# Last depthwise unit of a fused convolution kernel: results loaded in halves, an affine formed ahead, three weights issued later, a sigmoid by Exp

## The chip, the cores and the metric

The kernel runs on one core of a Trainium2 chip. The metric is device time in microseconds of one execution; the runs shown are the median of three. A profile is one further execution, recorded by the hardware profiler. The engines are PE (TensorE, matmuls; PEld are its weight loads), DVE (VectorE), ACT (ScalarE), POOL (GpSimd) and SP (SyncE, which only issues DMAs). ACT and POOL issue DMAs too. L1425 is line 1425 of the kernel before.

## The reference, cut to what matters

Four layers work on x of shape (4, 384, 64, 64) in float32; each is x + f(gn(x)), with gn a group norm. The change lies in layer 2:

```python
# layer 2, on x after the group norm; bn is a norm over batch and pixels, per channel
kw = softmax(bn(...))                       # two numbers for each batch, from the means of x
y3 = bn(depthwise 3x3 of x)
y5 = bn(depthwise 5x5 of x)
y1 = x * c1_w + c1_b                        # per channel
tok = bn(kw0 * y3 + kw1 * y5 + y1)
gp = tok.mean(over pixels)
gh = gelu(bn(gp @ cg_w1))
gates = sigmoid(bn(gh @ cg_w2))             # one number for each batch and channel
tok = tok * gates
h1 = gelu(bn(tok @ cm_w1)); h2 = bn(h1 @ cm_w2)
out = gate * (tok + h2) + (1 - gate) * x
```

Layer 0 is an attention, layer 1 a filter in the frequency domain, layer 3 a dynamic depthwise 7x7 convolution; they are not touched.

## The kernel before, in words

The kernel is one program of four phases. `phase_a` computes layers 0 and 1. `phase_b` computes the two depthwise convolutions of layer 2 and the sum tok before its norm. `phase_ef` forms tok's norm and the gates and does the two dense products of layer 2. `phase_g` does layer 3. A tile framework decides the order of the instructions on each engine from priorities and dependencies, and sets the semaphores; a DMA waits, by a ring of eight completion semaphores, for one some eight DMAs earlier. Each engine, and SP's queue of DMAs, works strictly in its order.

`phase_b` works in twelve units of 32 channels. For a unit, 16 steps of `conv53` do two channels each: TensorE multiplies strips of the image (z) with Toeplitz matrices made from the taps (L1425), ACT copies both results out of PSUM (L1434, L1436), DVE takes statistics (L1439), and after every fourth step ACT issues a store of 1 MiB (L1441) to a scratch tensor d in DRAM. So a unit has four such stores; that of steps 0 to 3 holds its channels 0 to 7, and so on. The layout in the unit is by image row, so the results come back by channel: `load_results` (L1482) reads a quarter of the rows of all 32 channels and 4 batches in one DMA of 1 MiB to 128 partitions (partition = 32 x batch + channel, pieces of 1 KiB).

`conv_norms` turns the statistics into the factors s (for the two convolutions) and the offset s0. `unit_tok` (L1491) then forms tok for a unit, in four parts of 1024 pixels: ACT forms x * c1_w + s0 for 512 pixels into PSUM (L1503), DVE adds the one convolution's result (L1512) and then the other's with a sum over the pixels (L1514), into x's own buffer; for each 1024 pixels ACT squares with a sum (L1524), and issues a store of tok (L1531, 512 KiB). For all units but the last this is spread over the steps of the next unit's convolutions. The results go into a pool of three buffers (`bc_p`), and the fourth load waits for the first to be free. For the last unit there is no next one. Its four results are loaded after its last store, into buffers of `bx_p` (six buffers of 8 KiB in each partition, which also hold x of three units, two buffers each), and `unit_tok` runs alone:

```python
            self.results = [self.load_results(UNITS - 1, i, self.bx_p, "x") for i in range(4)]
            self.conv_norms(UNITS - 1, behind)
            for _ in self.unit_tok(UNITS - 1):
                pass
            self.tok_stats()
```

`tok_stats` (L1533) sums up. At its start `phase_ef` issues three weights from ACT (L1601 to L1603, by `weight`, L335): cm_w1 (1.15 MiB), cg_w1 (36 KiB) and cg_w2 (36 KiB). Then come tok's norm (`bn_scale_shift`, with L374 Ln and L375 Exp for the inverse root), the matmuls with cg_w1 (L1613) and cg_w2 (L1620, with statistics L1622 and L1623), the sigmoid (L1627), and its products with the norm's scale and offset, at and ct (L1630, L1631). Sigmoid is not in the table of functions that holds Ln and Exp, so ACT loads a table before it and `ln_exp` loads the other again after it (L344).

The blocks of the dense product follow: SP loads tok for 1024 pixels (L1655, e_tok for two thirds of the channels and a part of z for the last third, in DMAs of 32 partitions and 128 KiB) and x (L1665, e_x, 1.5 MiB), DVE applies at and ct (L1656) and scales e_x (L1684), and TensorE multiplies with cm_w1 (h_s, L1671). 16 such blocks take about 500 us.

Of the kernel before, what the change touches and what calls it, by code (L numbers as in the profile page):

```python
# [30 lines left out]
P = 128  # L31
# [251 lines left out]
class _Builder:  # L283
# [930 lines left out]
    def phase_b(self):  # L1214
# [5 lines left out]
        with ExitStack() as ctx:  # L1220
# [13 lines left out]
            self.unit_x = [[] for _ in range(UNITS)]  # L1234
            first, strips, behind = self.unit_strips(0), self.unit_strips(1), None
            next(first)
            for u in range(UNITS):
                st = self.bt_p.tile([P, 2, 16, 6], F32, tag="st", name="st")
                tok = self.unit_tok(u - 1) if u else first
                for n in range(16):  # L1240
# [19 lines left out]
                    if not u and n in (1, 3):  # L1260
                        next(strips)
                    if n == 14 and not u:
                        for _ in tok:
                            pass
# [8 lines left out]
                behind, before = st, tok  # L1273
            self.results = [self.load_results(UNITS - 1, i, self.bx_p, "x") for i in range(4)]
            self.conv_norms(UNITS - 1, behind)
# [206 lines left out]
    def load_results(self, u, i, pool=None, tag="d"):  # L1482
# [6 lines left out]
        return d  # L1489

    def unit_tok(self, u):  # L1491

        nc = self.nc
        s, s0 = self.tok_s
        results, self.results = self.results, None
        behind = None
        for i in range(4):
            d = results[i]
            o = self.unit_x[u][i // 2][:, i % 2 * 1024 : i % 2 * 1024 + 1024]
            for h in range(2):  # L1500
                part = slice(h * 512, (h + 1) * 512)
                m = self.psum.tile([P, 512], F32, tag="t", name="tok_m", bufs=2)
                nc.scalar.activation(  # L1503
                    m, o[:, part], AF.Identity, bias=s0, scale=self.vec("c1_w")[:, u : u + 1]
                )
                if h == 0 and behind is not None:
                    self.square_and_store(u, *behind)
                    if len(results) == 3:
                        results.append(self.load_results(u, 3))
                mv, ov = (t.rearrange("p (y n) -> p y n", n=P) for t in (m, o[:, part]))  # L1510
                of = lambda v: d[:, 4 * h : 4 * h + 4, v]
                nc.vector.scalar_tensor_tensor(mv, of(1), s[:, 1:2], mv, ALU.mult, ALU.add)  # L1512
                k = 2 * i + h
                nc.vector.scalar_tensor_tensor(  # L1514
                    ov, of(0), s[:, 0:1], mv, ALU.mult, ALU.add, accum_out=self.total[:, u, k : k + 1]
                )
                yield
            behind = i, d, o
        self.square_and_store(u, *behind)

    def square_and_store(self, u, i, d, o):

        nc = self.nc
        nc.scalar.activation(  # L1524
            d.rearrange("p y v n -> p (y v n)")[:, 0:1024],
# [65 lines left out]
    def phase_ef(self, strips):  # L1591
        tc, nc = self.tc, self.nc
        with ExitStack() as ctx:
# [6 lines left out]
            io = first.enter_context(tc.tile_pool(name="e_io", bufs=2))  # L1600
            w1 = self.weight(ep, "cm_w1_t")  # L1601
            cg1 = self.weight(ep, "cg_w1_t")
            cg2 = self.weight(ep, "cg_w2_t")  # L1603

# [14 lines left out]
            for j in range(NJ):  # L1619
# [3 lines left out]
                nc.vector.bn_aggr(mv[:, j], st)  # L1623
            ga, gc = self.bn_scale_shift("cg2", mv[:, :, 0], mv[:, :, 1], self.vec("cg_g2"), self.vec("cg_b2"))
            for j in range(NJ):
                gates = self.sm([P, B], "gates")
                last = nc.scalar.activation(  # L1627
                    gates, z[:, j], AF.Sigmoid, bias=gc[:, j : j + 1], scale=ga[:, j : j + 1]
                )
                nc.vector.tensor_scalar(self.at[:, j, :], gates, a[:, j : j + 1], None, ALU.mult)  # L1630
                nc.vector.tensor_scalar(self.ct[:, j, :], gates, c[:, j : j + 1], None, ALU.mult)  # L1631


            self.ln_exp(last)
            stay = self.sm([P, B], "stay")
# [719 lines left out]
```

## Time and profile before

| what | value |
|---|---|
| time, median of 3 runs | 4648.23 us (4632.54 to 4652.59) |
| the profiled execution's own time | 4666.46 us |
| its span, first to last instruction | 4664.7 us |
| granted TensorE clock, mean | 0.969 |
| PE busy | 4356.6 us, 93% of the span |
| DVE, ACT, POOL busy | 61%, 43%, 17% |
| last conv store issued (L1441) | at 2969.97 us |
| first of the four c_d loads issued (L1485) | at 2973.88 us |
| last sum of unit_tok ends (L1514) | at 2998.13 us |
| first matmul of h_s (L1671) | at 3016.59 us |

Times inside the execution count from the start of its span. [...]the share is an average over stages, so the stretch around the change has to be read by itself. In rows of a timeline the engine's name with a q behind it is its sequencer, which issues the DMAs.

### The profile page before, as it was taken

The page shows a single profiled execution, that of the slowest core. Times are in us where ns is not written, and L with a number is a line of the kernel's source. Part 1 is how long each engine was busy: PE and PEld are TensorE (multiplying, and loading weights), DVE is VectorE, ACT ScalarE, POOL GpSimd, SP SyncE. Part 2 cuts the span into 40 slices and gives each one's busy share as a digit, 9 for nine tenths or more (in the row PEclk, how much of TensorE's full clock was granted, in tenths as well). Part 3 has the DMA queues.
Part 4 walks back from the last instruction along what each step waited for, and adds up shares of the span by engine and source line. Part 5 has one row for each costly group of instructions (what it writes and reads, how often), then busy time and mean ns, then how long its engine had stood idle before and what let it go on. Part 6 is the DMA issues. An engine that isn't in the chain of part 4 may idle for free.

```text
span 4664.7 us, 49796 instructions
## 1 busy us (share of the span) xinstructions
PE 4356.6 (93%) x18445; PEld 2415.0 (52%) x18445; DVE 2856.1 (61%) x4680; ACT 1991.0 (43%) x2913; POOL 810.8 (17%) x784
## 2 busy tenths in 40 slices
PE   7899999999999999998988899699999999888998
PEld 2233444334443444443538898444444444588987
DVE  6766566655666445554877888755541113777898
ACT  3444344444444443343535666411115333664442
POOL 1000000000000000000005566200000000245764
PEclk9999999999999999998989999799999999998999
DMA  4301211111111211112317999866655333796896
GB/s 141 114 33 50 84 68 68 53 63 48 61 68 46 71 37 59 50 61 82 127 64 248 315 336 331 298 257 254 257 225 212 140 144 134 280 348 234 264 316 223
DMA packets 284320, 730.36 MB, mean 157 GB/s; under 512 B 22331, under 2 KB 122790, under 8 KB 272806
## 3 DMA queue, kind: packets, MB, share of 16 engines
q1 hardware_dynamic: 213096, 407.56, 27.4%
q0 software_dynamic: 38880, 173.96, 9.9%
q10 hardware_dynamic: 32094, 145.57, 7.8%
q8 instruction: 149, 2.44, 0.2%
q14 instruction: 101, 0.83, 0.1%
HBM read 433.13 MB, written 293.86 MB: 156 GB/s over the span
## 4 chain that ended last, share of the span: by engine, by line
PE 70%; DVE 14%; DMA 8%; issue 3%; ACT 3%; POOL 1%; SPq 0%; ACTq 0%; DVEq 0%; POOLq 0%
PE av L933 11%; PE h_m L1792 11%; PE h_s L1671 11%; PE conv_m L1425 5%; PE sc_s L815 5%; PE proj_m L969 4%; DVE acc L1138 4%; PE t_m L1059 4%; PE conv_m L2187 3%; PE av L838 3%; PE out_m L1162 2%; PE out_m L1161 2%; PE back_m L1084 2%; DMA in_raw<-raw 2%; DMA x_in<-in_x 1%
## 5 line engine op out<-in xcount | busy, mean ns | idle before, releaser
L823 ACT ACTIVATE probs<-sc_s 128x1024 f32<-128x1024 f32 x512 | 497.2, 1021 | 698.5 <-PE av L933 597.9
L933 PE MATMUL av<-probs,vt 128*128 128x512 f32 x1536 | 723.9, 608 | 0.0
L1138 DVE SCALAR_TENSOR_TENSOR acc<-band,vecs,acc 128x512 f32<-128x512 f32 x708 | 496.2, 745 | 44.8 <-POOL band L1097 39.7
L1425 PE MATMUL conv_m<-toep,z 128*128 128x192 f32 (+1 forms) x2304 | 446.5, 351 | 21.7 <-DVE z L1354 11.9
L933 PEld LDWEIGHTS av<-probs,vt 128*128 128x128 f32 x1536 | 279.0, 193 | 343.3 <-issue 339.6
L1792 PE MATMUL h_m<-f_h,cm_w_t 128*128 128x512 f32 x1008 | 436.1, 595 | 7.4 <-ACT f_h L1729 7.4
L1425 PEld LDWEIGHTS conv_m<-toep,z 128*128 128x128 f32 x2304 | 402.6, 195 | 45.5 <-ACT d_o L1436 15.5
L2187 PE MATMUL conv_m<-toep,z 128*128 128x128 f32 x3072 | 383.7, 282 | 23.3 <-DVE toep L2174 13.8
L2187 PEld LDWEIGHTS conv_m<-toep,z 128*128 128x128 f32 x3072 | 370.3, 199 | 25.9 <-DVE toep L2174 10.0
L1671 PE MATMUL h_s<-e_tok,cm_w_t 128*128 128x512 f32 x768 | 362.8, 595 | 4.1 <-DVE e_tok L1656 4.1
L1792 PEld LDWEIGHTS h_m<-f_h,cm_w_t 128*128 128x128 f32 x1008 | 192.4, 191 | 250.6 <-issue 240.0
L815 PE MATMUL sc_s<-q,k 32*128 32x512 f32 x2048 | 307.2, 642 | 15.4 <-ACT probs L823 15.3
L1406 POOL TENSOR_TENSOR toep<-w,band 128x1280 f32<-128x1280 f32 x96 | 278.3, 2899 | 200.0 <-PE conv_m L1425 187.6
L1059 PE MATMUL t_m<-w_in_t,xb 128*128 128x384 f32 x768 | 281.1, 501 | 2.6 <-DVE coef L1076 2.4
L969 PE MATMUL proj_m<-xm,w_proj_t 128*128 128x512 f32 x576 | 271.2, 610 | 5.7 <-DVE xm L908 4.9
L1678 ACT COPY e_h<-h_s 128x1024 f32<-128x1024 f32 x96 | 97.3, 1013 | 400.1 <-PE h_s L1671 400.1
L1680 DVE BATCH_NORM_STATS2 h_st<-e_h 128x6 f32<-128x512 f32 x192 | 123.5, 685 | 219.3 <-ACT e_h L1678 219.3
L1671 PEld LDWEIGHTS h_s<-e_tok,cm_w_t 128*128 128x128 f32 x768 | 146.5, 191 | 188.2 <-issue 183.5
L976 DVE SCALAR_TENSOR_TENSOR x_res<-proj_m,bn_c,x_res 128x512 f32<-128x512 f32 x96 | 71.7, 747 | 241.0 <-PE proj_m L969 240.9
L1059 PEld LDWEIGHTS t_m<-w_in_t,xb 128*128 128x128 f32 x768 | 143.6, 193 | 141.3 <-issue 62.8
L1671 PE MATMUL h_s<-z,cm_w_t 128*128 128x512 f32 x384 | 196.7, 594 | 0.0
L838 PE MATMUL av<-probs,vt 128*32 128x512 f32 x1536 | 188.6, 603 | 4.6 <-DVE av_t L867 4.6
(464 smaller groups left out, 6336.4 us busy)
## 6 DMA issues: line engine op xcount, KB each, us to landing
d<-d_o ACTq DMA_DIRECT2D x48, 1024.0 KB
c_d<-d SPq DMA_DIRECT2D x48, 1024.0 KB
hid<-e_h ACTq DMA_DIRECT2D x16, 3072.0 KB
f_h<-hid SPq DMA_DIRECT2D x14, 3072.0 KB
x_in<-in_x SPq DMA_DIRECT2D x96, 256.0 KB
x_res<-in_x SPq DMA_DIRECT2D x32, 768.0 KB
xa<-x_res POOLq DMA_DIRECT2D x32, 768.0 KB, 3.7
xa_out<-xa SPq DMA_DIRECT2D x32, 768.0 KB
```

Of the source, the lines that this page charges most:

```text
L815: nc.tensor.matmul(s[:, g], lhsT=k4[32 * g : 32 * g + 32, c], rhs=q[i][32 * g : 32 * g + 32], start=True, stop=True,)
L823: nc.scalar.activation(p[:, h * 1024 : (h + 1) * 1024], s[:, 2 * h : 2 * h + 2].rearrange("p a b -> p (a b)"), AF.Exp, scale=0.25,)
L838: nc.tensor.matmul(av[k][quarter(g)], lhsT=vt[:, 4 * c + v, quarter(s)], rhs=p[:, v * 512 : (v + 1) * 512], start=c == 0 and not before, s ...
L933: nc.tensor.matmul(av[0], lhsT=vt[:, 4 * c + v, :], rhs=p[:, v * 512 : (v + 1) * 512], start=c == 0 and v == 0, stop=c == 7 and v == 3,)
L969: nc.tensor.matmul(m, lhsT=self.w_proj[:, j, o * P : (o + 1) * P], rhs=xm[:, j], start=j == 0, stop=j == NJ - 1,)
L1059: nc.tensor.matmul(m[:, 0:C], lhsT=xb[:, j], rhs=self.w_in[:, j, :], start=j == 0, stop=j == NJ - 1,)
L1138: nc.vector.scalar_tensor_tensor(out, src(j, k), w, done, ALU.mult, ALU.add)
L1406: eng.tensor_tensor(t, self.w53[:, at : at + 160].rearrange("p (m n) -> p m n", n=8).unsqueeze(2).to_broadcast([P, 20, 8, 8]), band.rearra ...
L1425: nc.tensor.matmul(m[:, c * 256 + to : c * 256 + to + 64 * (k1 - k0)], lhsT=self.z_[:, at : at + P], rhs=t[:, 10 * c + k0 : 10 * c + k1].r ...
L1671: nc.tensor.matmul(s[:, v, :], lhsT=w1[:, j, o * P : (o + 1) * P], rhs=t[j][:, v * 512 : (v + 1) * 512], start=j == 0, stop=j == NJ - 1,)
L1792: nc.tensor.matmul(m, lhsT=w2[:, o, j * P : (j + 1) * P], rhs=h[o][:, v * 512 : (v + 1) * 512], start=o == 0, stop=o == 5,)
L2187: nc.tensor.matmul(m[:, ch % 4 * P : (ch % 4 + 1) * P], lhsT=self.z_[:, at : at + P], rhs=t[:, 8 * c + 2 * i : 8 * c + 2 * i + 2].rearrang ...
```

## The change

In the last unit the four results are loaded in two halves of the channels. `load_half` reads 16 of the 32 channels, with one DMA for each batch: 16 partitions, 8 rows of 1 KiB each, 128 KiB. The first halves (channels 0 to 15, stored after steps 3 and 7) are put into the program after steps 8, 9, 12 and 15 of the last unit, into the same `bx_p` buffers; the second halves take the place of the old loads. So four DMAs become 32 of the same bytes in total. For the last unit, x * c1_w + s0 is formed ahead of the parts, in place in x's buffer and for 1024 pixels at a time; DVE then adds to it in place, and PSUM is not used. The three weights of `phase_ef` are issued from ACT behind the last unit's third square, the two small ones first. The sigmoid becomes 1 / (1 + exp(-v)): scale and offset are negated on DVE, ACT runs Exp, DVE adds one and takes the reciprocal; both table loads go.

```diff
--- before.py
+++ after.py
@@ -1232,7 +1232,7 @@
             for n in range(LEAD + 2):
                 self.matrices53(n)
             self.unit_x = [[] for _ in range(UNITS)]
-            first, strips, behind = self.unit_strips(0), self.unit_strips(1), None
+            first, strips, behind, last = self.unit_strips(0), self.unit_strips(1), None, []
             next(first)
             for u in range(UNITS):
                 st = self.bt_p.tile([P, 2, 16, 6], F32, tag="st", name="st")
@@ -1259,6 +1259,10 @@
                         next(tok, None)
                     if not u and n in (1, 3):
                         next(strips)
+                    if u == UNITS - 1 and n in (8, 9, 12, 15):
+                        last.append(self.bx_p.tile([P, 2 * 8 * P], F32, tag="x", name="c_d"))
+                        d = last[-1] = last[-1].rearrange("p (y v n) -> p y v n", v=2, n=P)
+                        self.load_half(u, len(last) - 1, d, 0)
                     if n == 14 and not u:
                         for _ in tok:
                             pass
@@ -1271,7 +1275,9 @@
                         if n == 15:
                             strips = coming
                 behind, before = st, tok
-            self.results = [self.load_results(UNITS - 1, i, self.bx_p, "x") for i in range(4)]
+            self.results = last
+            for d, i in zip(self.results, range(4)):
+                self.load_half(UNITS - 1, i, d, 1)
             self.conv_norms(UNITS - 1, behind)
             for _ in self.unit_tok(UNITS - 1):
                 pass
@@ -1488,21 +1494,39 @@
         )
         return d
 
+    def load_half(self, u, i, d, half):
+
+        at = 16 * half
+        for b in range(B):
+            self.nc.sync.dma_start(
+                d[32 * b + at : 32 * b + at + 16].rearrange("p y v n -> p y (v n)"),
+                self.d53[u][8 * i : 8 * i + 8, b, at : at + 16].rearrange("y c v n -> c y (v n)"),
+            )
+
     def unit_tok(self, u):
 
         nc = self.nc
         s, s0 = self.tok_s
         results, self.results = self.results, None
-        behind = None
+        behind, last = None, u == UNITS - 1
+        if last:
+            for x in self.unit_x[u]:
+                for k in range(2):
+                    x_k = x[:, k * 1024 : k * 1024 + 1024]
+                    nc.scalar.activation(
+                        x_k, x_k, AF.Identity, bias=s0, scale=self.vec("c1_w")[:, u : u + 1]
+                    )
         for i in range(4):
             d = results[i]
             o = self.unit_x[u][i // 2][:, i % 2 * 1024 : i % 2 * 1024 + 1024]
             for h in range(2):
                 part = slice(h * 512, (h + 1) * 512)
-                m = self.psum.tile([P, 512], F32, tag="t", name="tok_m", bufs=2)
-                nc.scalar.activation(
-                    m, o[:, part], AF.Identity, bias=s0, scale=self.vec("c1_w")[:, u : u + 1]
-                )
+                m = o[:, part]
+                if not last:
+                    m = self.psum.tile([P, 512], F32, tag="t", name="tok_m", bufs=2)
+                    nc.scalar.activation(
+                        m, o[:, part], AF.Identity, bias=s0, scale=self.vec("c1_w")[:, u : u + 1]
+                    )
                 if h == 0 and behind is not None:
                     self.square_and_store(u, *behind)
                     if len(results) == 3:
@@ -1511,17 +1535,18 @@
                 of = lambda v: d[:, 4 * h : 4 * h + 4, v]
                 nc.vector.scalar_tensor_tensor(mv, of(1), s[:, 1:2], mv, ALU.mult, ALU.add)
                 k = 2 * i + h
-                nc.vector.scalar_tensor_tensor(
+                self.last_sum = nc.vector.scalar_tensor_tensor(
                     ov, of(0), s[:, 0:1], mv, ALU.mult, ALU.add, accum_out=self.total[:, u, k : k + 1]
                 )
                 yield
             behind = i, d, o
+        self.third_square = self.last_square
         self.square_and_store(u, *behind)
 
     def square_and_store(self, u, i, d, o):
 
         nc = self.nc
-        nc.scalar.activation(
+        self.last_square = nc.scalar.activation(
             d.rearrange("p y v n -> p (y v n)")[:, 0:1024],
             o,
             AF.Square,
@@ -1598,9 +1623,10 @@
             first = ctx.enter_context(ExitStack())
             ep = first.enter_context(tc.tile_pool(name="e_const", bufs=1))
             io = first.enter_context(tc.tile_pool(name="e_io", bufs=2))
-            w1 = self.weight(ep, "cm_w1_t")
-            cg1 = self.weight(ep, "cg_w1_t")
-            cg2 = self.weight(ep, "cg_w2_t")
+            with tc.issue_after(self.third_square.ins):
+                cg1 = self.weight(ep, "cg_w1_t")
+                cg2 = self.weight(ep, "cg_w2_t")
+                w1 = self.weight(ep, "cm_w1_t")
 
             a, c = self.bn_scale_shift("bn_ar", *self.over_batches("ar", self.mvt), self.vec("ar_g"), self.vec("ar_b"))
             gp = self.sm([P, NJ, B], "gp")
@@ -1622,16 +1648,17 @@
                 nc.vector.bn_stats(st, z[:, j])
                 nc.vector.bn_aggr(mv[:, j], st)
             ga, gc = self.bn_scale_shift("cg2", mv[:, :, 0], mv[:, :, 1], self.vec("cg_g2"), self.vec("cg_b2"))
+            for v in (ga, gc):
+                nc.vector.tensor_scalar(v, v, -1.0, None, ALU.mult)
             for j in range(NJ):
                 gates = self.sm([P, B], "gates")
-                last = nc.scalar.activation(
-                    gates, z[:, j], AF.Sigmoid, bias=gc[:, j : j + 1], scale=ga[:, j : j + 1]
-                )
+                nc.scalar.activation(gates, z[:, j], AF.Exp, bias=gc[:, j : j + 1], scale=ga[:, j : j + 1])
+                nc.vector.tensor_scalar(gates, gates, 1.0, None, ALU.add)
+                nc.vector.reciprocal(gates, gates)
                 nc.vector.tensor_scalar(self.at[:, j, :], gates, a[:, j : j + 1], None, ALU.mult)
                 nc.vector.tensor_scalar(self.ct[:, j, :], gates, c[:, j : j + 1], None, ALU.mult)
 
 
-            self.ln_exp(last)
             stay = self.sm([P, B], "stay")
             nc.vector.tensor_scalar(stay, self.gate, -1.0, 1.0, ALU.mult, ALU.add)
             self.gx, self.gn, self.gh, self.g0 = (self.coef(k) for k in ("gx", "gn", "gh", "g0"))
```

`issue_after` places an instruction behind a given one in its engine's order.

## Prediction

> **What bounds the kernel now.** I read the windows view first: where is TensorE idle around the change? Columns: stretch, its length, then busy time and count for PE, PEld, DVE, ACT and POOL, granted clock, DMA share, GB/s.
>
> ```profile
> 2970.00:3016.60 46.60, 4.64 (x25) 3.73 (x25) 23.73 (x82) 18.97 (x34) 0.58 (x1) 0.54 0.97 300
> 3016.60:3513.00 496.40, 496.40 (x1151) 219.73 (x1152) 259.14 (x406) 96.98 (x96) 11.28 (x16) 1.00 0.66 244
> ```
>
> For 46.6 us TensorE has almost nothing to do; then it is full for 496 us at a DMA share of 0.66. What moves the end of the first stretch moves the end of the kernel by as much, and nothing outside that stretch is touched by more than its last neighbours. The change can thus never win more than 46.6 us, 1.0%. In the stretch no engine is half busy, but the 16 DMA engines are at 0.97.
>
> Next the timeline of that stretch (start us, length us, engine, line, what; in brackets the idle time before it and what ended it).
>
> ```profile
> 2969.97 0.33 ACTq L1441 DMA_DIRECT2D d<-d_o  x1
> ...
> 2973.92 0.36 ACTq L335 DMA_DIRECT2D cm_w_t<-in_cm_w_t  x1
> ...
> 2982.75 1.41 DVE L1512 SCALAR_TENSOR_TENSOR tok_m<-c_d,cn_s,tok_m 128x512 f32<-128x512 f32 x2 [8.62 <-DMA c_d<-d]
> ...
> 2997.38 0.75 DVE L1514 SCALAR_TENSOR_TENSOR unit_x<-c_d,cn_s,tok_m 128x512 f32<-128x512 f32 x1
> ...
> 3009.41 1.53 DVE L1684 TENSOR_SCALAR e_x<-e_x,gx,gn 128x1024 f32<-128x1024 f32 x2 [2.39 <-DMA e_x<-x]
> ...
> 3013.52 1.28 ACT L1627 ACT_TABLE_LOAD   x1
> ...
> 3016.59 3.78 PE L1671 MATMUL h_s<-e_tok,cm_w_t 128*128 128x512 f32 x4 [4.08 <-DVE e_tok L1656]
> ```
>
> The last store of conv results leaves at 2969.97; four loads c_d of 1 MiB follow at 2973.88, beside the 1.15 MiB weight cm_w1. VectorE waits 8.62 us for the first c_d, then works from load to load until 2998.13 (2997.38 + 0.75). From there 18.46 us of small steps lead to the first h_s matmul at 3016.59. So two terms count: the end of VectorE's last sum, and the tail of 18.46.
>
> Last, the rate of the loads, by windows without other large traffic:
>
> ```profile
> 2449.00:2455.00 6.00, 4.86 (x17) 4.45 (x18) 5.14 (x7) 0.65 (x2) 5.14 (x3) 0.72 1.01 240
> ...
> 2980.00:2989.00 9.00, 0.00 (x0) 0.00 (x0) 5.24 (x11) 3.33 (x5) 0.00 (x0) 0.50 1.11 349
> ```
>
> In the upper row only the 32-partition loads unit_x run (ten, 128 KiB each): 240 GB/s with the DMA engines full. In the lower only the 128-partition c_d: 349 GB/s, though its pieces are 1 KiB and those of unit_x 4 KiB. Fewer partitions, slower.
>
> [...]from 2976 to 2979 the weight's queue moved 0.92 MB and that of c_d 0.27 MB[...]. [...]Exp ends at 3013.51, the load starts at 3013.52.
>
> **The change, part by part.**
>
> *Loads in halves.* Four c_d loads of 1 MiB (128 partitions, 3.0 us each at 349 GB/s, 12 us) become 32 loads of 128 KiB, each to 16 partitions. At half of 240 GB/s one takes 1.09 us[...]. I take 1.17 (112 GB/s), so all 32 take 37.4 us of DMA time. Only the first halves can lie beside the convs, and the SP queue is in order. By the instruction order of the changed kernel, SP now runs: three c_d of unit 10, the first load of half 0, unit 10's fourth c_d, then all 31 others, and only then the e_tok loads. The first load waits for the store of 2948.32, so it starts its data near 2953.3; unit 10's fourth c_d (3.07 us) is held behind it and lands near 2957.9. It is needed at 2960.6, so the convs should not notice (bounds: 0 to +3 us; taken 0). Then 15 loads of half 0 remain, 17.55 us. While an ACT store runs beside them, [...](three tok stores, 1.65 us each, loss 0.45 each)[...] (two d stores, 2.9 us each, loss 1.7 each): 4.75 us together. 2957.9 + 17.55 + 4.75 = 2980.2. The last d store still lands near 2974, but half 1 stands behind half 0 on the ring, so its data start at 2980.2, not at 2974.9.
>
> Half 1 is 4 x 4.68 = 18.7 us, plus 0.45 for each of the three tok stores that fall into it: the fourth tile is complete near 3000.8 with 0.2 us of completion. VectorE needs 2.74 us per tile (2982.75 to 2985.49 for the first), less than the 5.1 between tiles, so it is paced by the loads: 3000.8 + 2.74 = 3003.5. Before: 2998.13. **+5.4 us.**
>
> *Affine ahead, in place.* Eight 128x512 activations (0.77 us each, L1503) become four of 128x1024 (1.25 us each, by L1334), all issued once s0 is there at 2974.33: done at 2979.3. The loads hide it; if they came early it would set VectorE's start at 2975.6. The 3.2 us for which VectorE waited on L1503 go; they go into waiting for c_d. L1512 with all operands in SBUF: 0.745 us by L1138, as before.
>
> *Weights behind the third square.* cm_w1, cg_w1 and cg_w2 leave near 2998.7 instead of 2973.92. Gain: c_d is no longer held by cm_w1 from 2976 to 2979. That is already in the sum, as I charge no weight there. Cost: three DMA issues on ACT (1.5 us) ahead of the fourth square, which waits for VectorE until 3003.5 anyway: 0. At 1.15 MiB beside the e_tok loads the weight needs some 5 us, so near 3005; its first matmul is near 3020. If that cover went, h_s would wait for it. The e_tok loads (eight and two z, 5.5 us at 240 GB/s) come behind half 1 on SP: near 3008, needed near 3018.
>
> *The tail.* In the compiled order the three e_x operations (L1684) no longer stand between the small statistics. Before, cg_z was ready at 3009.37 and the last L1623 ended at 3012.92; without them three rounds of matmul and bn_stats (0.85 us each) end at 3011.46: -1.46. Gate: the table load for Sigmoid (3013.52 to 3014.80) goes, but c is ready only at 3014.09 and two negations follow (0.2 each), so Exp starts at 3014.5 instead of 3014.82: -0.31. Then add (0.2), reciprocal (0.17 by L2007, some 0.25 with its wait) and their interleaved copies: +0.48. Tail: 18.46 - 1.46 + 0.17 = **17.17**. The second table load removed (3016.04) is on no path.
>
> Sum: 3003.5 + 17.17 = 3020.7 for the first h_s, against 3016.59: **+4.1 us**. The profiled execution took 4666.46 us, its span 4664.7; with the change 4670.6 and 4668.8. The runs shown have a median of 4648.23, 0.4% below the profiled one; on it I put the same 4.1: **4652.3 us**.
>
> **Rivals.**
>
> [...] Then half 0 is done before 2974 but for its fourth tile, which waits for unit 10's last tok store (2967.25); half 1 gives its first tile near 2977.5 and VectorE runs without a stop for 4 x 2.74 = 11 us, to 2988.5; plus 17.17: 3005.7, -11 us, 4637. For: the 1 KiB packets of c_d need only 0.05 us of an engine. Against: 240 GB/s of the 32-partition loads, which also had several in flight.
>
> *Stalled loads hold the engines*: [...] Then stores add their full time: five before 2980 take 9.0 us instead of 4.75, three later 3.9 instead of 1.35, the last d store itself lands later, and unit 10's late c_d stalls the convs by up to 3 us. 4.1 + 4.2 + 2.5 + 3 = +14 us, 4662. It leaves the band of no change only if one 16-partition load takes over 1.79 us (31 loads in line, 3.1 us for each 0.1; (23.2 - 4.1) / 3.1 = 6.2 steps above 1.17).
>
> *Half 0 is not ahead at all*: SP reaches it only at 2974, because of its waits. Then 37.4 us run after 2974.9: VectorE ends near 3016, +17 us, 4665. Against: the buffers of unit 9 are free, and the stores it waits for left at 2939 and 2948.
>
> **Numbers.** 0.5%, 23.2 us, is about what a measurement of this kernel can tell from no change; three runs spread over 20 us. Forecast 0.58, [...]engines held 0.13, not ahead 0.04. Each carries some 9 us of scatter. From 4634 (the fast rival less a third of its scatter) to 4667 (the slow ones plus half) about 0.8 is inside. Faster than the band needs the fast rival and 12 us of luck: 0.04. Slower needs a load above 1.79 us, or a slow rival and bad luck: 0.04. No change: 0.92.
>
> **What would show it.** Right: half-load windows at 105 to 125 GB/s with the DMA share near 1; VectorE before L1512's successor idle until DMA four times; its last sum near 3003; no e_x between the cg statistics; one table load less before the gates; TensorE full from the first h_s on. Wrong: VectorE waiting once only and ending near 2989[...]; holes in the convs between 2955 and 2970 (engines held); any difference that arises after 3100.

## The result and the profile after

| | median | lowest to highest | runs |
|---|---|---|---|
| before | 4644.88 us | 4632.54 to 4658.41 | 11 |
| after | 4661.55 us | 4651.10 to 4666.72 | 11 |

The ratio after to before is 1.0025, with a 95% interval of 1.0013 to 1.0037: slower by 6 to 17 us, and inside the band of no change. The median after lies in the range of 4634 to 4667 us that was forecast. The profiled execution after took 4662.01 us; its span is 4660.2 us, shorter than the 4664.7 of before. The spans mislead here: the two executions are 9.2 us apart at the second conv store of the last unit (2948.32 before, 2939.16 after), before the first half load is issued, and 10.8 us at the last (2969.97 before, 2959.14 after). So all times below count from the issue of **the last d store**, written +t.

| | last sum ends | tail | first h_s matmul |
|---|---|---|---|
| before | +28.17 | 18.46 | +46.63 |
| predicted | +33.5 | 17.17 | +50.7 |
| after | +36.89 | 16.91 | +53.80 |

The stretch became 7.2 us longer, where 4.1 were predicted. 7.2 lies inside the interval of the runs, near its lower end; the medians are 16.7 us apart, and what they differ by beyond the 7.2 is not accounted for. The windows view of after over that stretch and over the h_s stage (columns: stretch, length, busy and count of PE, PEld, DVE, ACT and POOL, clock, DMA share, GB/s):

```profile
2959.14:3012.94 53.80, 4.63 (x24) 3.71 (x24) 21.93 (x83) 16.09 (x28) 0.59 (x1) 0.53 1.04 225
3012.94:3509.70 496.76, 496.76 (x1152) 219.59 (x1152) 261.64 (x413) 96.14 (x95) 11.27 (x16) 1.00 0.67 247
```

TensorE is full from the first h_s on, for 496.76 us against 496.40: nothing is won or lost there. In the stretch the DMA engines are as full as before (1.04 against 0.97) but move 225 GB/s instead of 300. Next the windows of the half loads, in times when nothing else of size runs:

```profile
2965.00:2972.00 7.00, 0.00 (x0) 0.00 (x0) 0.00 (x0) 2.97 (x3) 0.00 (x0) 0.50 1.17 117
2972.00:2980.00 8.00, 0.00 (x0) 0.00 (x0) 2.73 (x6) 0.00 (x0) 0.00 (x0) 0.50 1.18 117
```

The engines are booked in full at a third of the 349 GB/s of the whole loads. At 117 GB/s one half load of 128 KiB takes 1.12 us. The DMA view gives the packets of SP's queue, for whole loads before (2980 to 2989) and then for half loads (2965 to 2976): their number, MB, and the share of the 16 engines' time that they took.

```profile
q1 hardware_dynamic: 3054, 3.08, 108.1%
```

```profile
q1 hardware_dynamic: 1420, 1.29, 117.5%
```

Most packets are of 1 KiB in both. On average one occupies its engine for 51 ns in the whole loads (108.1% of 16 x 9 us, over 3054) and for 146 ns in the half loads (117.5% of 16 x 11 us, over 1420). The timeline shows what VectorE makes of it (start, length, engine, line; in brackets the idle time before and its cause):

```profile
2959.14 0.33 ACTq L1447 DMA_DIRECT2D d<-d_o  x1
...
2977.27 1.42 DVE L1536 SCALAR_TENSOR_TENSOR unit_x<-c_d,cn_s,unit_x 128x512 f32<-128x512 f32 x2 [13.96 <-DMA c_d<-d]
...
2981.72 1.41 DVE L1536 SCALAR_TENSOR_TENSOR unit_x<-c_d,cn_s,unit_x 128x512 f32<-128x512 f32 x2 [1.70 <-DMA c_d<-d]
...
2985.97 1.41 DVE L1536 SCALAR_TENSOR_TENSOR unit_x<-c_d,cn_s,unit_x 128x512 f32<-128x512 f32 x2 [1.49 <-ACT c_d L1549]
...
2990.56 0.38 ACTq L335 DMA_DIRECT2D cm_w_t<-in_cm_w_t  x1
...
2993.27 1.41 DVE L1536 SCALAR_TENSOR_TENSOR unit_x<-c_d,cn_s,unit_x 128x512 f32<-128x512 f32 x2 [4.55 <-DMA c_d<-d]
...
2995.27 0.75 DVE L1538 SCALAR_TENSOR_TENSOR unit_x<-c_d,cn_s,unit_x 128x512 f32<-128x512 f32 x1
...
3010.82 0.60 ACT L1655 ACTIVATE gates<-cg_z,cg_c,cg_a 128x4 f32<-128x4 f32 x2 [0.82 <-DVE cg_c L1652]
...
3012.94 2.07 PE L1698 MATMUL h_s<-e_tok,cm_w_t 128*128 128x512 f32 x2 [3.94 <-DVE e_tok L1683]
```

VectorE is idle four times, once for each tile; the third wait is put down to ScalarE's square of the tile before, of which the operation reads nothing, the others to the loads. The first, 13.96 us, is longer than the 8.62 of before although half of that tile was loaded ahead. No table load stands ahead of the gate's Exp at 3010.82, no e_x between the statistics, and the weight cm_w1 leaves at 2990.56, not in the midst of the loads.

### The profile page after: what moved, and what is told of

Its sections match the earlier page's. It is cut to its first block, busy times and chain, and to the rows that moved or that the text cites. A ratio compares the mean times of both kernels' runs of the same rounds, so it can differ in the third digit from the quotient of the medians.

```text
span 4660.2 us, 49828 instructions
## 1 busy us (share of the span) xinstructions
PE 4349.4 (93%) x18445; PEld 2412.2 (52%) x18445; DVE 2858.8 (61%) x4688; ACT 1982.0 (43%) x2907; POOL 811.4 (17%) x784
## 4 chain that ended last, share of the span: by engine, by line
PE 69%; DVE 14%; DMA 8%; ACT 4%; issue 4%; POOL 1%; SPq 1%; ACTq 0%; DVEq 0%; POOLq 0%
PE av L933 11%; PE h_s L1698 11%; PE h_m L1819 9%; PE conv_m L1431 6%; PE proj_m L969 4%; PE sc_s L815 4%; PE t_m L1059 4%; DVE acc L1138 4%; PE conv_m L2214 3%; PE av L838 3%; PE out_m L1162 2%; PE out_m L1161 2%; PE back_m L1084 2%; DMA g_h<-h 1%; DMA x_in<-in_x 1%
```

## The experiments

All are read by the same marks. "Whole" is the changed kernel with c_d loaded in four DMAs of 1 MiB after the last store. Ratios are to the kernel before, run on the same chip; where none stands, there was one run and its profile.

| run | first tile starts | last sum ends | tail | first h_s | ratio, 95% interval |
|---|---|---|---|---|---|
| before | +12.78 | +28.17 | 18.46 | +46.63 | |
| after | +18.12 | +36.89 | 16.91 | +53.80 | 1.0025 [1.0013, 1.0037] |
| whole | +9.70 | +23.03 | 16.93 | +39.95 | 0.9991 [0.9980, 1.0003] |
| every second partition | +12.31 | +26.27 | 16.93 | +43.20 | 0.9998 [0.9988, 1.0009] |
| tok stores from POOL | +17.64 | +34.26 | 16.93 | +51.19 | 1.0012 [1.0005, 1.0020] |
| wide halves | +11.29 | +22.07 | 17.21 | +39.27 | 0.9991 [0.9981, 1.0001] |
| whole, early weights | +12.73 | +26.10 | 16.93 | +43.03 | |
| whole, Sigmoid | +9.53 | +22.84 | 17.11 | +39.95 | |
| whole, affine by tile | +9.46 | +25.34 | 21.58 | +46.92 | |
| halves alone | +22.64 | +41.22 | 17.01 | +58.23 | |
| two tiles ahead, first try | +11.45 | +22.26 | 17.20 | +39.46 | 0.9984 [0.9975, 0.9993] |
| two tiles ahead, order held | +9.16 | +22.17 | 17.10 | +39.27 | 0.9983 [0.9970, 0.9995] |

The marks are of one profile each. Wide halves and the first try with two tiles, which ran in nearly the same order, agree within 0.2 us in all four. The whole times scatter by 20 us: the intervals of after and whole do not overlap, which fits the marks, but those of whole, of every second partition and of wide halves include 1.

### The halves undone

```diff
-                    if u == UNITS - 1 and n in (8, 9, 12, 15):
...
-                        self.load_half(u, len(last) - 1, d, 0)
-            self.results = last
-            for d, i in zip(self.results, range(4)):
-                self.load_half(UNITS - 1, i, d, 1)
+            self.results = [self.load_results(UNITS - 1, i, self.bx_p, "x") for i in range(4)]
```

> The change with its halves undone: the last unit's four results are loaded whole again (four loads of 128 partitions, 1 MiB each), everything else of the change stays. I count from the issue of the last conv store to the end of VectorE's last sum, and from there to the first h_s (the tail). Before: 28.2 + 18.5 = 46.6 us; changed kernel: 36.9 + 16.9 = 53.8 us. Theory (the narrow loads cost it): first data at +4.9, 3.0 us per load, 1.3 us lost per tok store, VectorE 2.74 us after the fourth: last sum near +23, tail 16.9, together about 40, 14 below the changed kernel and 7 below before; time about 4638. Rival (affine ahead, late weights or the Exp gate cost it): stays above 50, time as the changed kernel.

Measured: first h_s at +39.95. **The halves cost 13.9 us** (53.80 less 39.95), and the rest of the change gains 6.7 (46.63 less 39.95). The groups of VectorE, for the kernel before and then for this one (busy time, mean ns, then idle time and what ended it):

```profile
L1512 DVE SCALAR_TENSOR_TENSOR tok_m<-c_d,cn_s,tok_m 128x512 f32<-128x512 f32 x8 | 5.9, 754 | 12.5 <-DMA c_d<-d 9.3 <-ACT tok_m L1503 3.2
```

```profile
L1530 DVE SCALAR_TENSOR_TENSOR unit_x<-c_d,cn_s,unit_x 128x512 f32<-128x512 f32 x8 | 5.7, 750 | 7.8 <-DMA c_d<-d 5.5 <-ACT c_d L1543 1.9 <-issue 0.4
```

The waits fell from 12.5 to 7.8 us together, and that for the affine from 3.2 to nothing. The 1.9 us that the view puts to ScalarE's square stand ahead of the fourth tile, which reads nothing of that square. In the trace the packets of the fourth load end at 2974.6, 1.0 us before that tile starts, and those of the first three end 0.9 to 1.0 us before theirs; so this wait is for the load too.

### The same 32 loads on every second partition

The channels of the last unit are computed evens first, then odds, so that a half is every second partition:

```diff
-                d[32 * b + at : 32 * b + at + 16].rearrange("p y v n -> p y (v n)"),
+                d[32 * b + half : 32 * b + 32 : 2].rearrange("p y v n -> p y (v n)"),
```

> The changed kernel, with the last unit's channels taken in another order: even ones first, then odd. A half-load still has 16 partitions, 128 KiB and 1 KiB pieces, and there are still 32 of them, but they land on every second partition of a block of 32 instead of on 16 neighbours[...]. The statistics need two small copies more. Theory[...]: 0.56 us per load instead of 1.13, rate of half-load windows near 230 GB/s, last sum near +20, together near 37, time about 4636. Rival (16 partitions, or the number of loads, bind as such): rate stays near 117 GB/s and the last sum near +37.

Measured: last sum 10.6 us earlier than with consecutive partitions, with the same loads, bytes and pieces. The windows view and one row of the timeline:

```profile
2975.00:2983.00 8.00, 0.00 (x0) 0.00 (x0) 2.52 (x5) 2.07 (x2) 0.00 (x0) 0.50 0.69 201
```

```profile
2975.44 5.11 SPq L1521 DMA_DIRECT2D c_d<-d  x8
```

The rate is 201 GB/s with the engines only 0.69 busy, so the DMA engines no longer bind. The new bound is SP: it issues eight loads in 5.11 us, 0.64 us each, one right behind the other, and 128 KiB in 0.64 us are 205 GB/s. That is why it stayed short of the expectation, together with a wait of 3.1 us before the fourth tile, ahead of which SP stood still for 3.4 us until a store of tok had landed. So 10.6 of the 13.9 us that the halves cost go with which partitions a load reaches. What in the chip makes sixteen consecutive ones slower, at 117 GB/s, no run shows.

### The tok stores of the last unit from another queue

```diff
-        nc.scalar.dma_start(self.tok[u, :, :, i * 1024 : i * 1024 + 1024].rearrange("b c n -> (b c) n"), o)
+        eng = nc.gpsimd if u == UNITS - 1 else nc.scalar
+        eng.dma_start(self.tok[u, :, :, i * 1024 : i * 1024 + 1024].rearrange("b c n -> (b c) n"), o)
```

> The changed kernel with one edit: the four tok stores of the last unit are issued from POOL instead of ACT, so they leave the ring of completion semaphores that SP's half-loads share with ACT's stores. In the changed kernel SP stood still for 7.0 us, from 2979.7 to 2986.7, until tok store 0 had landed, before it issued the fourth tile's half-loads, and the half-loads' queue was empty from 2984.5 to 2987. Theory (the ring's wait is what was not in the sum): no such wait, fourth tile and last sum about 3 us earlier, +33.7 instead of +36.9. Rival (the store held the DMA engines, and the loads would have waited anyway): last sum stays within 1 us of +36.9.

Measured: last sum at +34.26 instead of +36.89. The waits of SP's queue from 2978 to 2988 (waited for: total us, times, longest), after and then here:

```profile
SPq L1501 <- DMA tok<-unit_x: 7.0, 1, 7.0
SPq L1501 <- DMA c_d<-d: 2.7, 2, 1.9
```

```profile
SPq L1501 <- DMA c_d<-d: 5.5, 3, 2.9
```

In the changed kernel SP stands still for 7.0 us before a half load, until a store of tok has landed that ACT had issued at 2980.16. The load has nothing to do with that store: both take a completion semaphore from the one ring of eight (in the trace of after, the DMAs of SP and ACT name the same eight semaphores, those of POOL eight others, and this store and this load name one and the same). Most of the 7 us, until 2984.5, is covered by loads still under way. The last sum comes 2.6 us earlier, 2.1 of them after the first tile, and these are what the wait costs, if the other queue of these stores changes nothing else. The other 0.5 lie before the first tile, where none of the moved stores had left yet. They go with another difference: the second and the last conv store of the unit are 21.67 us apart here and 19.98 in after, at a granted clock of 0.88 against 1.00 in the first part of that stretch, so the first halves had 1.7 us more.

### Halves as wide loads

As the run on every second partition, and the scratch of the last unit is laid out by halves, so that one DMA of 64 partitions (every second) and 512 KiB takes the place of four:

```diff
-        for b in range(B):
-            self.nc.sync.dma_start(
-                d[32 * b + at : 32 * b + at + 16].rearrange("p y v n -> p y (v n)"),
-                self.d53[u][8 * i : 8 * i + 8, b, at : at + 16].rearrange("y c v n -> c y (v n)"),
-            )
+        self.nc.sync.dma_start(
+            d[half::2].rearrange("p y v n -> p y (v n)"),
+            self.d53[u][half, 8 * i : 8 * i + 8].rearrange("y b c v n -> (b c) y (v n)"),
+        )
```

> Halves by even and odd channels[...], and the scratch tensor of the last unit is laid out by halves, so that one load takes a half of a tile for all four batches: 64 partitions in steps of 2, 512 KiB, eight loads instead of 32. Theory: [...]1.5 us per load at 349 GB/s; half 1 keeps ahead of VectorE, whose 11 us of sums then run without a stop from about +6.6: last sum near +18, tail 17 to 17.7, together near 35, 11.5 us below before; time about 4633. Rival (VectorE then waits for something else, s0 or stores): last sum above +22.

Measured: last sum at +22.07, no better than the rival's bound. Windows, then the group of VectorE:

```profile
2976.00:2980.00 4.00, 0.00 (x0) 0.00 (x0) 2.87 (x7) 0.03 (x1) 0.00 (x0) 0.50 1.08 358
```

```profile
L1558 DVE SCALAR_TENSOR_TENSOR unit_x<-c_d,cn_s,unit_x 128x512 f32<-128x512 f32 x8 | 5.7, 750 | 7.1 <-DMA c_d<-d 7.1
```

Now the loads run at 358 GB/s and VectorE waits once, 7.1 us for the first tile, then works 10.7 us without a stop. What was to be gained from reading ahead went into the first tile, which starts at +11.29, later than the +9.70 with whole loads. The last d store landed 6.6 us after its issue here, 3.9 with whole loads, read from the issue of the load that waits for it: stores of tok, loads of z and the halves run ahead of it or beside it, and the second halves wait for it. This run does not say which of these holds it.

### What the three other parts are worth

Each is the whole version with one part put back.

```diff
-            with tc.issue_after(self.third_square.ins):
-                cg1 = self.weight(ep, "cg_w1_t")
-                cg2 = self.weight(ep, "cg_w2_t")
-                w1 = self.weight(ep, "cm_w1_t")
+            w1 = self.weight(ep, "cm_w1_t")
+            cg1 = self.weight(ep, "cg_w1_t")
+            cg2 = self.weight(ep, "cg_w2_t")
```

> The changed kernel with c_d loaded whole (as in the run before) and the three weights issued where they were before the change, beside the c_d loads. Times are counted from the last d store, since the runs differ by some us before it; with whole loads and late weights the last sum ended at +23.0 and the first h_s began at +39.95. Theory of the prediction: cm_w1 (1.15 MiB in 9 KiB packets) takes some 3.3 us from the c_d loads, and VectorE is paced by them: last sum near +26.5, first h_s near +43.4. Rival: VectorE has slack beside the loads, and the weights' move is worth nothing: within 0.7 us of +23.0 and +39.95. If the theory holds, the move of the weights carries half or more of what the change without the halves gains.

Measured: +26.10 and +43.03. **The weights' move is worth 3.1 us**; the theory holds, though this is a little less than half of the 6.7.

```diff
-            for v in (ga, gc):
-                nc.vector.tensor_scalar(v, v, -1.0, None, ALU.mult)
...
-                nc.scalar.activation(gates, z[:, j], AF.Exp, bias=gc[:, j : j + 1], scale=ga[:, j : j + 1])
-                nc.vector.tensor_scalar(gates, gates, 1.0, None, ALU.add)
-                nc.vector.reciprocal(gates, gates)
+                last = nc.scalar.activation(
+                    gates, z[:, j], AF.Sigmoid, bias=gc[:, j : j + 1], scale=ga[:, j : j + 1]
+                )
...
+            self.ln_exp(last)
```

> The changed kernel with c_d loaded whole and the gate formed by Sigmoid again, with its two table loads, instead of Exp, add and reciprocal; order of the other instructions the same. The tail from the last sum to the first h_s was 16.92 with Exp. Theory of the prediction: the table load that goes (1.28 us) was nearly all beside other work, and add and reciprocal cost more than it saves, 0.17 net: tail near 16.75 with Sigmoid. Rival: the table load lies on the path in full: tail near 18.0. The last sum does not move (+23.0).

Measured: a tail of 17.11 with Sigmoid against 16.93 with Exp. Neither number of the expectation came: **Exp gains 0.18 us**, too little for the rival and of the other sign than the theory. The timeline of ScalarE with Sigmoid, and then with Exp:

```profile
3001.71 0.20 ACT L375 ACTIVATE cg_a<-cg_a 128x3 f32<-128x3 f32 x1
3001.93 1.28 ACT L1647 ACT_TABLE_LOAD   x1
3003.23 0.60 ACT L1647 ACTIVATE gates<-cg_z,cg_c,cg_a 128x4 f32<-128x4 f32 x2
```

```profile
2992.12 0.20 ACT L375 ACTIVATE cg_a<-cg_a 128x3 f32<-128x3 f32 x1
2993.16 0.60 ACT L1649 ACTIVATE gates<-cg_z,cg_c,cg_a 128x4 f32<-128x4 f32 x2 [0.83 <-DVE cg_c L1646]
```

From the start of L375 to the gate it is 1.52 us with the table load and 1.04 with VectorE's five small operations: 0.48 saved. From the gate to the first e_tok product it is 0.94 (3004.17) and 1.25 (2994.41): 0.31 given back.

```diff
-        behind, last = None, u == UNITS - 1
+        behind, last = None, False
```

> The changed kernel with c_d loaded whole and the affine of the last unit formed tile by tile into PSUM, as before the change, instead of ahead in place. Theory: with whole loads the tiles come every 2.95 us and VectorE needs 2.7, so ScalarE's two affines of 0.77 us per tile, in line with its squares and stores, cost 0.5 to 2 us: last sum +23.5 to +25. Rival of no effect: +23.0 within 0.4. Rival of the whole wait that the kernel before showed (3.2 us on this line): +26.2. Two operations on e_x fall between the cg statistics in this order, so its tail may be longer than 16.92 by 1 to 2 us; that is not the affine's.

Measured: last sum at +25.34, so **the affine ahead is worth 2.3 us**, a little more than the theory's 0.5 to 2. VectorE's group shows what comes back:

```profile
L1530 DVE SCALAR_TENSOR_TENSOR tok_m<-c_d,cn_s,tok_m 128x512 f32<-128x512 f32 x8 | 5.9, 755 | 9.7 <-DMA c_d<-d 6.5 <-ACT tok_m L1521 3.1
```

Of these 3.1 us of waiting, 2.3 reach the end. The tail of 21.58 is another matter, and longer than the 1 to 2 us that I had expected: the order puts e_x operations before and between the cg statistics, and the timeline shows VectorE idle at the first of them.

```profile
2996.86 0.81 DVE L1705 TENSOR_SCALAR e_x<-e_x,gx,gn 128x1024 f32<-128x1024 f32 x1 [3.76 <-issue]
2997.59 0.15 DVE L410 BATCH_NORM_STATS2 cg_st<-cg_z 24x6 f32<-24x4 f32 x1
```

The timeline names no cause for these 3.76 us, but the waits of SP's queue do (window 2996 to 2997):

```profile
SPq L1676 <- DMA e_x<-x: 4.5, 1, 4.5
```

SP's next load waits for the load of e_x, which lands at 2996.78, 0.08 us before VectorE's operation starts; in the kernel before, such an operation had waited 2.39 us for its load. So e_x at this place in the order costs 4.65 us here, more than any part of the change without the halves. The three parts make 5.6 us of the 6.7. The rest goes with the order too: in the next run, without e_x between the statistics, the tail is 1.45 us shorter than in the kernel before.

### The halves alone

The kernel before with `load_half` and its calls, and nothing else.

> The kernel before with the loads in halves alone: weights beside them as before, affine tile by tile as before, Sigmoid gate. Counted from the last d store, the changed kernel had its last sum at +36.9 and the first h_s at +53.8; the kernel before +28.2 and +46.6. Theory: the 16-partition loads pace VectorE, so the affine has all the time it needs and costs nothing here (with whole loads it cost 2.3 us); the weights (3.1 us with whole loads) still take DMA time from the loads[...]: last sum near +40, and a tail near 17.1 (Sigmoid, no e_x between the statistics): first h_s near +57. Rival: [...]the two other parts of the change are worth nothing beside halves: +36.9 within 1 us, first h_s near +54.

Measured: +41.22 and +58.23, near the theory's numbers. Beside halves the two other parts do not become worthless: the last sum comes 4.3 us later than in the changed kernel. This goes with the weights that leave early. The group shows no wait on the affine, which is hidden behind the loads:

```profile
L1527 DVE SCALAR_TENSOR_TENSOR tok_m<-c_d,cn_s,tok_m 128x512 f32<-128x512 f32 x8 | 5.7, 752 | 26.1 <-DMA c_d<-d 24.6 <-ACT c_d L1539 1.5
```

### A version meant to be faster than both

Wide halves, but only the first two tiles read their first half ahead:

```diff
-                    if u == UNITS - 1 and n in (8, 9, 12, 15):
+                    if u == UNITS - 1 and n in (8, 9):
```

> A version meant to beat both: even channels of the last unit first, scratch laid out by halves, loads of 64 partitions and 512 KiB (as in the run with wide halves), but only the first two tiles have their first half loaded ahead; the halves of tiles 3 and 4 all come behind the last d store. In the run with wide halves the half loads ahead and other loads beside them made the last d store land 6.6 us after its issue (3.9 with whole loads), and the first tile was ready at +11.3; then VectorE ran without a stop, 10.7 us. Theory: with less ahead the store lands after some 4.5 us, the first tile is there near +8, VectorE is not held afterwards (5 half loads of 1.5 us stand for tiles 2 to 4), last sum near +19, first h_s near +36, ten us less than before the change: some 4638 beside 4648, ratio 0.998. Rival: it was not the halves ahead but the tok stores and z loads that held the last d store: it lands after 6 us or more, first tile at +10.5 or later, last sum +21.5 or later, first h_s +38.5 or later.

Measured: +22.26 and +39.46, the rival's numbers, but this run decides nothing between the two. The framework issued the first halves of tiles 3 and 4 ahead of the last d store's landing all the same, and the store landed after 6.6 us again. So it is a second measurement of the version with wide halves; its ratio is 0.9984 [0.9975, 0.9993]. Once more with the order held by `issue_after` on SP's own queue:

```diff
+            self.second = self.load_half(UNITS - 1, 0, last[0], 1)
+            with tc.issue_after(self.second.ins):
+                self.load_half(UNITS - 1, 1, last[1], 1)
+                for i in (2, 3):
...
+                    for half in range(2):
+                        self.load_half(UNITS - 1, i, last[i], half)
...
+                            first_z = j == 2 and q == 2 and b + i == 0
+                            with tc.issue_after(self.second.ins) if first_z else nullcontext():
```

The last two lines put one load of z, which stood ahead of the last d store's landing, behind these loads as well.

> The run with two tiles ahead once more, now with the order held on SP: in the run before this one the first halves of tiles 3 and 4 were still issued ahead of the last d store's landing (at -4.4 and +4.1 us), so its edit did not change what the chip ran. Here the six half loads (second halves of tiles 1 and 2, both halves of tiles 3 and 4) are issued in a row, 64 partitions and 512 KiB each, behind the last d store. Theory: with fewer loads beside it the store lands after 4 to 5 us instead of 6.6; first tile near +8.3, VectorE paced by neither loads nor buffers after it (10.7 us): last sum near +19.5, first h_s near +36.6, some 4640 beside 4650, ratio 0.998. Rival: two z loads and unit 10's tok stores still stand ahead of the store, which lands after 6 us or more: last sum +21.5 or later, first h_s +38.5 or later, as in the run with wide halves. Second rival: with more loads behind the store the loads pace VectorE, last sum +21 or later though the store lands early.

Measured: the store landed 4.8 us after its issue and the first tile came at +9.16, near what the theory has. Fewer half loads and one load of z less stand ahead of the store here, and the run does not take the two apart. Yet the last sum ends at +22.17, which is the second rival. The timeline of VectorE:

```profile
2976.93 1.41 DVE L1564 SCALAR_TENSOR_TENSOR unit_x<-c_d,cn_s,unit_x 128x512 f32<-128x512 f32 x2 [4.94 <-DMA c_d<-d]
2979.60 1.41 DVE L1564 SCALAR_TENSOR_TENSOR unit_x<-c_d,cn_s,unit_x 128x512 f32<-128x512 f32 x2
2982.75 1.41 DVE L1564 SCALAR_TENSOR_TENSOR unit_x<-c_d,cn_s,unit_x 128x512 f32<-128x512 f32 x2 [0.39 <-DMA c_d<-d]
2987.18 1.41 DVE L1564 SCALAR_TENSOR_TENSOR unit_x<-c_d,cn_s,unit_x 128x512 f32<-128x512 f32 x2 [1.68 <-DMA e_tok<-tok]
```

The first tile is early, and the 2 us won come back as waits before tiles 3 and 4. (A load of e_tok is named for the last, but the operation reads c_d, and SP's queue waits for a load of c_d until 2987.06, 0.12 us before it starts.) Whole loads, wide halves and both versions here all reach h_s between +39.27 and +39.95. The last two are faster than before by an interval that leaves out 1, by about 8 us; that they beat the plain whole loads is not shown.

## Why the prediction was right, and where it was short

**The bound: right.** Sixteen consecutive partitions set the rate, 117 GB/s where the whole loads have 349; the loads, not VectorE, paced the last unit. I took 1.17 us for a half load; half of 240 GB/s gives 1.09, and the 0.08 on top was my estimate, which no trace of before shows. It is 1.12. The run on every second partition, with 201 GB/s for the same 32 loads, shows that it is which partitions they reach, not their number.

**The first rival (0.25), half loads at the 349 GB/s of whole ones: refuted**, with the engines fully booked at 117 GB/s. **Half 0 not ahead: refuted**: SP issued its first load at 2943.12, 16 us ahead of the last d store.

**Stalled loads hold the engines: half right.** No conv stalled: from the last d store of unit 10 to the last of unit 11 it took 39.88 us, with whole loads 39.87. But stores and loads cost each other more than I charged (0.45 us for each tok store and 1.7 for each d store, an estimate of mine that no trace of before shows), and this is the first term that was mis-sized. The first tile was to be ready at +15.1 (2980.2 + 4.68 + 0.2, less 2969.97); it came at +18.12, **3.0 us later**. Two windows of after show where half 0 starts:

```profile
2946.00:2949.00 3.00, 1.62 (x9) 1.55 (x10) 2.76 (x7) 3.00 (x8) 1.92 (x1) 1.00 1.05 341
2949.00:2951.00 2.00, 2.00 (x13) 1.92 (x12) 2.00 (x7) 2.00 (x5) 0.00 (x0) 1.00 1.21 149
```

Until 2949, unit 10's whole load has the engines (341 GB/s); only then do half loads dominate. That is -10.1, where the sum had -12.1. Of these 2.0 us, 1.7 are no cost of the loads. The sum counts from the profile before, where the second and the last conv store of the unit are 21.65 us apart; in after they are 19.98 apart. The first part of that stretch, before and then after, shows why: the same matmuls at another granted clock.

```profile
2948.32:2962.81 14.49, 12.05 (x58) 11.04 (x57) 13.94 (x31) 8.25 (x18) 5.90 (x3) 0.88 0.70 241
```

```profile
2939.16:2952.04 12.88, 10.44 (x59) 9.69 (x58) 12.04 (x26) 8.21 (x18) 5.93 (x3) 1.00 0.93 272
```

The run with tok stores from POOL has the clock of before there (0.88), and its first tile still comes only at +17.64, so the clock is the smaller part of the 3.0 us.

The larger part is the time that the first halves lost. Counting back from the first tile, half 0 is over near +13.4 (four loads of 1.12 and 0.2 earlier), so its 15 loads of 1.12 us (16.8) took 23.5: 6.7 us were lost beside stores and in waits, 4.75 had been taken. The sum put the waits of SP for ACT's stores at nothing. In after they are (window 2957.5 to 2966):

```profile
SPq L1501 <- DMA d<-d_o: 6.5, 2, 4.4
...
SPq L1501 <- DMA tok<-unit_x: 0.6, 1, 0.6
```

SP stood still for 4.4 us, until 2958.07, for one d store and for 2.1 us for the last, though these loads read nothing that the two stores write. In the ten us from 2953 the DMA view of after gives the two queues:

```profile
q10 hardware_dynamic: 579, 3.10, 80.2%
q1 hardware_dynamic: 565, 0.51, 19.6%
```

ACT's stores (q10) moved 3.10 MB and the half loads (q1) 0.51, or 51 GB/s, 0.44 of their own rate. That is near the 0.41 that my charge of 1.7 us leaves of a d store's 2.9, but since SP stood still for some 4 of these ten us it does not test that estimate. How much of the 6.7 us is sharing and how much is SP's wait stays open.

**From the first tile to the last sum: right by two errors.** I had 18.42 us and it took 18.77. The 18.42 has a slip: 2980.2 + 18.7 + 3 x 0.45 + 0.2 is 3000.5, not 3000.8, so it should read 18.1 and the whole step +3.8. I had no wait of SP on ACT's stores through the shared semaphores; it costs 2.1 us here, as this stretch took 16.62 with the tok stores on POOL. That figure is 1.8 below my 18.42: 0.3 are the slip, the loads were faster than 1.17 us, which is 0.6 over twelve of them, and the rest would be a smaller loss beside the tok stores than I took, which no run takes apart. The errors nearly cancel, which is luck.

**Affine ahead: right.** It costs nothing and, beside halves, gains nothing; with whole loads it gains 2.3 us. **Weights: right** in place and size: 3 us were named from the timeline, 3.1 measured. I charged no cost for the later weight, and h_s does not wait for it.

**The tail: right by two terms.** -1.46 for e_x was taken, and the run of halves alone, with Sigmoid and without e_x there, has 17.01, or -1.45. The gate was put at +0.17 and is -0.18: its start gains 0.48, not 0.31, since the two negations issue 0.1 us apart and not one after the other; add and reciprocal cost 0.31, not 0.48, as their copies interleave.

So of the 3.1 us by which the step of +4.1 was too small, 3.4 lie in the last sum (3.0 of them before the first tile) and -0.3 in the tail. One reading of the first view was not exact: VectorE is busy for 23.73 of the 46.60 us there, 51%, so one engine is half busy; nothing in the sum rests on it.

## What to carry to other kernels

Reading a tile ahead in halves asks first for halves that load as fast as the whole (here 64 of every second partition, 358 GB/s against 349), and even then the first h_s came just 0.7 us earlier here than with whole loads. Cut by consecutive partitions (117 GB/s), the half left for later took longer than the whole had taken, and a neutral-looking split cost 13.9 us where the rest of the change gained 6.7. Before moving a load forward, ask what runs beside it then: a store that the later loads depended on landed 6.6 us after its issue with wide halves instead of 3.9, and the shared ring of semaphores made SP wait 7.0 us for a foreign store. Compare two profiles from a mark just ahead of the change, not by their spans; here the spans had the wrong sign. Look at the granted clock up to the mark as well: 0.88 against 1.00 moved it by 1.7 us.

## What the runs showed of the hardware

- Which 16 partitions matters, not only how many: consecutive ones got 117 GB/s with the DMA engines fully booked, every second one 201 GB/s with the engines at 0.69, and 64 of every second one 358 GB/s. A packet to 16 consecutive partitions occupied its engine for 146 ns on average, one of the whole loads for 51 ns.
- SP took 0.64 us to issue a 128 KiB load to every second partition, eight in a row; with loads of this size the issuing queue then sets the rate (205 GB/s by that, 201 measured).
- A 1 MiB store landed 3.9 us after its issue with little beside it, 4.8 and 6.6 with loads and stores ahead of it or beside it.
